# A gated feed-forward layer on one NeuronCore: where the second batch's x is loaded, and where the last sum of sign blocks stands in its slot

## The chip, the cores and the metric

The kernel runs on 1 core of one Trainium2 chip. The metric is the device time of one execution in microseconds (us). A profiled execution gives the span from the first to the last instruction of the program; the execution's own time is a little longer than that span.

## The reference, cut to what matters

Four batches of 1024 tokens with 512 features each pass through one conditioned gated layer:

```
scale = cond @ norm_w.T + 1.0
ms = mean(x * x, axis=-1, keepdims=True)
h = x * (scale[:, None, :] * rsqrt(ms + 1e-6))
u = h @ up_w.T                        # 512 -> 2 * 2048
val, gate = split(u, 2, axis=-1)
h = val * gelu(gate, approximate=False)
hq = act_quant(h)                     # per token: round(h * 127 / max|h|), scaled back
wq = weight_quant(down_w)             # -1, 0, 1 times mean|down_w|
y = hq @ wq.T                         # 2048 -> 512
return y + x
```

Everything is float32 outside the kernel; x is 4 x 1024 x 512.

## The kernel before, in words

**Tiling.** The 2048 hidden features are cut into NJ = 16 groups of 128. One *slot* is the work on one group for one batch: the "up" product of 1024 tokens (two halves of 512) with the group's gate and value rows, a Gelu on ScalarE (ACT), and a multiplication on VectorE (DVE) that writes the slot of `H`. Batch 0 runs in 16 *plain* slots (`first_batch(j, sc)`, j = 3 to 15, with j = 0 to 2 written out ahead of it); there the up product is made of 12 float16 matmuls of 128x128 by 128x512 for a gate (`pg`) and 12 for a value (`pv`), for each half (`plain_half`). From batch 1 on a slot uses seven products of a Strassen-like scheme (`slot`, `product`).

**What else the plain slots of batch 0 do.** They prepare the weights that later batches reload: `w_load(j + 4)` brings a group's 512 KB of `up_w` (line L261), `w_range(j + 3)` takes its largest values on DVE (L269, L147, L275, L278), `w_scale` and `w_rows` scale it and split it into high and low float16 parts (ACT L295 and L319, DVE L320, and a transposing DMA L321), `s_sums` builds sums on GpSimd (POOL, L353 to L356), `s_all` splits them (ACT L365, POOL L369) and spills the result to `s_dram` (L373, three DMAs from group 8 on). They also round the down weights (`d_round`, DVE L439 and L440; `d_put`, ACT L449 and a transposing DMA L451 into `wd`).

**Batch 1's x.** From slot 6 on, four pieces `Tokens(1, a)` of 256 tokens are prepared, each in two slots. In the even slot 6 + 2a: `norm` (ACT L495, then POOL L466 and L467), `scale` (ACT L503, DVE L508), `sums` (POOL L516 to L519). In the odd slot after it: `high` (ACT L540), `low` (DVE L544), `turn` (a transposing DMA, L547). The load itself, 512 KB, is `Tokens.load` (L487), and `next_tokens(j)` issues it for the piece that begins in slot j + 1: in slots 7 and 9 near the front of the slot, behind `w_load`, in slots 5 and 11 late in it. Pieces 0, 2 and 3 share one buffer, tag `xn`; piece 1 uses `H[:, 11]`.

**What sets the order.** The order of each engine's instructions is written out by hand (`manual_schedule`): an engine runs its list in the order of the source. All transfers spoken of here are issued by SyncE's queue (SP) in that order, and an SP instruction that waits holds up all behind it. From slot 6 to slot 11 that order is: w10, spill 7, L321 of group 9, spill 8 (three); w11, x for slot 8, `wd`, turn 0, spill 9 (three), L321 of group 10; w12, spill 10, L321 of 11; w13, x for slot 10, `wd`, turn 1, spill 11, L321 of 12; w14, spill 12, L321 of 13; w15, `wd`, x for slot 12, turn 2. (w12 stands for the load of group 12.)

**PSUM banks.** A value product `pv` uses tag `E` with two banks. So the `pv` of a half waits for the DVE multiplication (L604) of the half two places before it.

**The down product of batch 0** is made in slots 10 to 13 of batch 1, one piece of 256 tokens in each (`Pair`, L832), from blocks of `wd` and four differences of them, T1 to T4. `d_sums((n,))` makes difference n, as two DVE subtractions of 128x1024 float8 elements (L462). `D_SUM_AT` gives each slot a tuple of those made early in the slot, behind `pair.sums()`, and a tuple of those made late, behind `pair.third`. T2 is read by `pair.third`, T3 by `pair.fourth`, T4 by `pair.fifth`. The planner in the loop over batches takes `D_SUM_US` for every difference off the slot's DVE time, early or late.

```
D_SUMS = [("T1", "B12", "B11"), ("T2", "B22", "T1"), ("T3", "B22", "B12"), ("T4", "B21", "T2")]
D_SUM_AT = {(1, 9): ((0,), (2,)), (1, 10): ((1,), (3,))}
TOKENS = {6: 0, 8: 1, 10: 2, 12: 3}
```

Of the kernel before, what the change touches and what calls it, by code (L numbers as in the profile page):

```python
# [8 lines left out]
F32 = mybir.dt.float32  # L9
# [9 lines left out]
P = 128  # L19
# [31 lines left out]
def glu_quant_kernel(  # L51
# [14 lines left out]
    TOK = 512  # L66
# [10 lines left out]
    wpool = ctx.enter_context(tc.tile_pool(name="work", bufs=2))  # L77
# [16 lines left out]
    H = cpool.tile([P, NSLOT, 2, TOK], F32, name="H")  # L94
# [45 lines left out]
    def h_slots(g, n=1):  # L140
        s = g % NSLOT
        return H[:, s : s + n]
# [73 lines left out]
    def cond_spread(dg, b0, b1, tag):  # L216
        n = b1 - b0
        pd = bank(tag, {"po": 3}.get(tag, 2), [P, B], f"pd_{b0}")[:, :n]
        PE.matmul(pd, ones[:n, :], dg, start=True, stop=True)
        return pd  # L220

    def cond_undo(pd, b0, b1):
        DVE.reciprocal(ux[:, b0:b1], pd)
        if b0 == 0:
            DVE.tensor_scalar(scT[:, :, 0], scT[:, :, 0], ux[:, 0:1], None, ALU.mult)
        DVE.tensor_copy(dx[:, b0:b1], pd)

    def cond_rows():

        for b in range(1, B):  # L230
            SP.dma_start(out=rows_dram[b].rearrange("(k p) -> p k", p=P), in_=scT[:, :, b])
# [27 lines left out]
    def w_load(j, ts=(1, 0)):  # L259
        if j > 2:  # L260
            SP.dma_start(out=wn(j), in_=up_v[j])  # L261
            return
        for t in ts:
            SP.dma_start(out=wn(j)[:, t], in_=up_v[j][:, t])

    def w_largest(j, t0=0, t1=2):
        t = slice(t0, t1)
        am = sm.tile([P, 2], F32, name=f"wam_{j}_{t0}", tag="wam")[:, t]
        DVE.tensor_reduce(am, wn(j)[:, t], AX.X, ALU.max, apply_absolute_value=True)  # L269
        return am  # L270
# [9 lines left out]
    def w_range(j, t0=0, t1=2):  # L280
        w_factor(j, w_largest(j, t0, t1), t0, t1)

    def w_gain(j):
        DVE.tensor_scalar(sg0[:, j, :], sw[:, j, :], dx[:, 0:1], None, ALU.mult)
# [5 lines left out]
    def w_scale(j, ts=(1, 0), eng=None):  # L290
        eng = eng or (ACT if j >= ROWS else POOL)
        for t in ts:
            w, r = wn(j)[:, t], iv[j][:, t : t + 1]
            if eng is ACT:
                ACT.activation(w, w, AF.Copy, scale=r)  # L295
            else:
                eng.tensor_scalar(w, w, r, 1.0, ALU.mult, ALU.mult)
# [49 lines left out]
    def s_sums(j):  # L347
        if j >= ROWS:
            v = wn(j).rearrange("p t (n f) -> p t n f", n=2)
            a11, a12, a21, a22 = v[:, 1, 0], v[:, 1, 1], v[:, 0, 0], v[:, 0, 1]  # L350
        else:
            a11, a12, a21, a22 = (wf(j)[:, n] for n in range(4))
        POOL.tensor_tensor(sf[:, 0], a21, a22, ALU.add)  # L353
        POOL.tensor_tensor(sf[:, 2], a11, a21, ALU.subtract)
        POOL.tensor_tensor(sf[:, 1], sf[:, 0], a11, ALU.subtract)
        POOL.tensor_tensor(sf[:, 3], a12, sf[:, 1], ALU.subtract)  # L356
# [61 lines left out]
    def d_load(n):  # L418
        c, u, _ = d_at(n)
        SP.dma_start(out=d_part(n), in_=down_w[c * P : (c + 1) * P, u * HF : (u + 1) * HF])  # L420
# [5 lines left out]
    def d_total():  # L426
        part = sm.tile([P, 1], F32, name="wpart", bufs=1)
        DVE.tensor_reduce(part, wsum, AX.X, ALU.add)
        return part
# [39 lines left out]
    class Tokens:  # L469


        def __init__(self, b, a, at=None, nx_at=None):
            self.b, self.a = b, a
            if at is None:
                if a == 1:
                    self.xn = H[:, 11]
                else:
                    self.xn = wpool.tile([P, 2, D], F32, name=f"xn_{b}_{a}", tag="xn", bufs=1)
                self.xt = wpool.tile([P, 4, HALF], F32, name=f"xt_{b}_{a}", tag="xt", bufs=1)
            else:  # L480
                v = h_slots(at, 2)
                self.xn = v[:, 0]
                self.xt = v[:, 1].rearrange("p h (n d) -> p (h n) d", n=2)
            self.nx_at = nx_at
# [111 lines left out]
    def plain_half(j, h, between=nothing):  # L596
        pg = bank(*(("A", 2) if h or j == 1 else ("B", 1)), name=f"pg_{j}_{h}")
        plain(j, 1, h, pg)
        t1 = wpool.tile([P, TOK], F32, name=f"g_{j}_{h}", tag="t1")
        ACT.activation(t1, pg, AF.Gelu, scale=gain(j, 1))  # L600
        between()
        pv = bank("E", 2, name=f"pv_{j}_{h}")
        plain(j, 0, h, pv)
        DVE.scalar_tensor_tensor(h_half(j, h), pv, gain(j, 0), t1, ALU.mult, ALU.mult)  # L604
# [80 lines left out]
    def pair_max(b, i, h):  # L685

        v = h_slots(b * NJ + 2 * i, 2)[:, :, h].rearrange("p j t -> p t j")
        m = m_view(b, h)
        if i == 0:
            return [lambda: DVE.tensor_reduce(m, v, AX.X, ALU.max, apply_absolute_value=True)]  # L690
        gm = []

        def largest():
            gm.append(wpool.tile([P, TOK], F32, name=f"gm_{b}_{i}_{h}", tag="gm", bufs=1))
            DVE.tensor_reduce(gm[0], v, AX.X, ALU.max, apply_absolute_value=True)  # L695

        return [largest, lambda: DVE.tensor_tensor(m, m, gm[0], ALU.max)]  # L697
# [260 lines left out]
    am = w_largest(0, 1, 2)  # L958
# [39 lines left out]
    TOKENS = {6: 0, 8: 1, 10: 2, 12: 3}  # L998
# [4 lines left out]
    toks = {}  # L1003

    def next_tokens(j):
        if j + 1 in TOKENS:
            toks[j + 1] = toks[j + 2] = Tokens(1, TOKENS[j + 1])
            toks[j + 1].load()

    def s_all(j):  # L1010
        s_high(j)
        s_low(j, POOL)
        s_spill(j)

    def first_batch(j, sc):

        if j + 4 < NJ:
            w_load(j + 4)
        for n in D_LOAD.get(j, ()):
            d_load(n)  # L1020
        if j in (7, 9):
            next_tokens(j)
        t = toks.get(j)
        odd = t is not None and j not in TOKENS
        n = j + 2
        rows = ROWS <= n < NJ
        if j + 1 < ROWS:
            s_sums(j + 1)
        elif rows:
            s_sums(n)  # L1030
        if j + 3 < NJ:
            w_range(j + 3)
            w_gain(j + 3)
        if j == 5:
            part = d_total()
        if j + 3 < ROWS:
            w_scale(j + 3)
        plain_half(j, 0)
        if j == 3:
            pd = cond_spread(dg, 1, B, "po")  # L1040
            cond_undo(pd, 1, B)
            cond_rows()
        pairs = PAIRS.get(j, ())
        for i, h in pairs[:2]:
            for f in pair_max(0, i, h):
                f()
        if j + 1 < ROWS:
            s_all(j + 1)
        if n < ROWS:
            w_turn(n)  # L1050
            w_high(n)
            w_evac(n)
            w_low(n)
        if t and not odd:
            t.norm()
        for m in D_ROUND.get(j - 1, ()):
            d_put(m)
        for m in D_ROUND.get(j, ()) if j > 5 else ():
            d_round(m)
        if t and not odd:  # L1060
            t.scale(sc)
            t.sums()
        if odd:
            t.high()
            t.low(DVE)
        if j not in (7, 9):
            next_tokens(j)
        if odd:
            t.turn()
        plain_half(j, 1)  # L1070
        if j == 5:
            d_mean(part)
        if rows and j + 1 >= ROWS:
            s_all(n)
        if ROWS <= j + 3 < NJ:
            w_scale(j + 3)
            w_rows(j + 3)
        if rows and j + 1 < ROWS:
            s_sums(n)
            s_all(n)  # L1080
        if j == 5:
            d_round(0)
        for i, h in pairs[2:]:
            for f in pair_max(0, i, h):
                f()
        for n in D_SUM.get(j, ()):
            d_sum(n)
        if j in (NJ - 3, NJ - 1):
            s_load_x(NJ + (j - NJ + 3) // 2)
            s_load_y(NJ + (j - NJ + 3) // 2)  # L1090
# [99 lines left out]
    DOWN = {10: 0, 11: 1, 12: 2, 13: 3}  # L1190
    SLOT_US = 9.07
    PAIR_US = 6.2 - 5.1
    D_SUM_AT = {(1, 9): ((0,), (2,)), (1, 10): ((1,), (3,))}
    D_SUM_US = 2.3
    OWN_US = 3.0

# [71 lines left out]
    for b in range(1, B):  # L1268
        dve, act = Filler(), Filler()
        gains(b)  # L1270
        am = am_tile(b - 1)
        dq = state[b - 1] = sm.tile([P, 2 * NA], F32, name=f"dq_{b}", tag="dq")
        last_pair = NJ // 2 - 1
        for h in range(2):
            add_pair(
                dve, act, b - 1, last_pair, h, (0, "xz"[h]),
                lambda now, h=h: token_max(b - 1, h, am),
# [36 lines left out]
        for j in range(NJ):  # L1314
            g = b * NJ + j
            down = b + 1 < B and j in DOWN
            if down:
                pair, a = pairs[j], DOWN[j]
                xrs = [down_load(b - 1, h, a) for h in range(2)]
            early_sums, late_sums = D_SUM_AT.get((b, j), ((), ()))  # L1320
            left = SLOT_US + PAIR_US * down - OWN_US + 0.4
# [77 lines left out]
    b = B - 1  # L1399
    am = am_tile(b)  # L1400
# [158 lines left out]
```

## Time and profile before

| | us |
|---|---|
| three runs | 739.97, 740.22, 744.1 |
| their median | 740.22 |
| the profiled execution, own time | 740.59 |
| its span | 738.8 |
| TensorE busy (matmul) | 725.0 |
| VectorE busy | 592.3 |
| ScalarE busy | 390.8 |
| GpSimd busy | 201.4 |

The granted TensorE clock is full in all 40 slices of the page. A plain slot's four products of 12 matmuls take 2.59 us each. Slot 6 begins at 86.6 us, slot 8 at 107.85, slot 10 at 128.6, slot 12 at 151.75; the second batch begins at 195.1 us, and its slots 9 and 10 lie from about 269 to 301 us. Busy shares are averages; what a stage costs is read from the waits of TensorE in it and from what came last before each of them.

### The profile page before, as it was taken

The page shows a single profiled execution, that of the slowest core. Times are in us where ns is not written, and L with a number is a line of the kernel's source. Part 1 is how long each engine was busy: PE and PEld are TensorE (multiplying, and loading weights), DVE is VectorE, ACT ScalarE, POOL GpSimd, SP SyncE. Part 2 cuts the span into 40 slices and gives each one's busy share as a digit, 9 for nine tenths or more (in the row PEclk, how much of TensorE's full clock was granted, in tenths as well). Part 3 has the DMA queues.
Part 4 walks back from the last instruction along what each step waited for, and adds up shares of the span by engine and source line. Part 5 has one row for each costly group of instructions (what it writes and reads, how often), then busy time and mean ns, then how long its engine had stood idle before and what let it go on. Part 6 is the DMA issues. An engine that isn't in the chain of part 4 may idle for free.

```text
span 738.8 us, 10217 instructions
## 1 busy us (share of the span) xinstructions
PE 725.0 (98%) x3700; PEld 363.2 (49%) x3700; DVE 592.3 (80%) x837; ACT 390.8 (53%) x639; POOL 201.4 (27%) x217
## 2 busy tenths in 40 slices
PE   7999999899999999999999999999999999999998
PEld 3545444344444445565444445666444444445844
DVE  6968687986989888897679898687678888764897
ACT  5757657566235676443434666453433665332274
POOL 1499467787010031460010030452020000000100
PEclk9999999999999999999999999999999999999999
DMA  6289849999623456757933446656933335444253
GB/s 235 75 314 189 255 142 248 255 232 206 215 89 105 127 104 173 184 139 179 225 103 102 135 101 171 157 146 165 227 103 103 106 97 106 107 103 98 88 185 114
DMA packets 163022, 114.68 MB, mean 155 GB/s; under 512 B 124950, under 2 KB 129943, under 8 KB 162972
## 3 DMA queue, kind: packets, MB, share of 16 engines
q1 hardware_dynamic: 162682, 113.70, 58.3%
q8 instruction: 29, 0.48, 0.3%
q10 hardware_dynamic: 290, 0.33, 0.1%
q14 instruction: 21, 0.17, 0.1%
HBM read 62.08 MB, written 23.09 MB: 115 GB/s over the span
## 4 chain that ended last, share of the span: by engine, by line
PE 92%; DMA 2%; DVE 2%; ACT 1%; POOL 1%; issue 1%; SPq 0%; DVEq 0%; ACTq 0%
PE A L561 33%; PE E L561 17%; PE pv L576 9%; PE pg L576 8%; PE B L561 8%; PE po L832 8%; PE po_end L781 4%; DMA H<-in_L_cond_up_w_dram 1%; PE pw L305 1%; PE po L781 1%; DMA H<-in_x_dram 1%; PE ptx L922 1%; PE po_B L832 0%; DVE wd L462 0%; PE pv L619 0%
## 5 line engine op out<-in xcount | busy, mean ns | idle before, releaser
L561 PEld LDWEIGHTS <-SXY 128*128 128x128 f16 x2016 | 197.2, 98 | 232.3 <-issue 0.6
L561 PE MATMUL A<-R,SXY 128*128 128x512 f16 x1152 | 266.2, 379 | 0.0
L561 PE MATMUL E<-R,SXY 128*128 128x512 f16 x576 | 140.0, 379 | 0.1
L659 DVE SCALAR_TENSOR_TENSOR H<-A,sg,t 128x512 f32<-128x512 f32 x48 | 36.0, 750 | 74.2 <-PE A L561 74.0
L711 POOL PARTITION_ALL_REDUCE am<-R x8 | 14.3, 1793 | 231.1 <-DVE R L697 231.1
L753 DVE TENSOR_TENSOR H<-H,am 128x1024 f32<-128x1024 f32 x64 | 76.2, 1217 | 0.0
L672 ACT ACTIVATE t<-t,sg 128x512 f32<-128x512 f32 x48 | 34.6, 721 | 70.9 <-DVE t L669 70.7
L576 PEld LDWEIGHTS <-SXY 128*128 128x128 f16 x438 | 42.9, 98 | 55.2 <-issue 4.8
L561 PE MATMUL B<-R,SXY 128*128 128x512 f16 x288 | 70.0, 379 | 0.0
L695 DVE TENSOR_REDUCE gm<-H 128x512 f32<-128x1024 f32 x56 | 69.0, 1232 | 1.0
L832 PE MATMUL po<-wd,R 128*128 128x256 fp8e4 (+1 forms) x448 | 56.9, 275 | 1.4 <-DVE wd L462 1.4
L576 PE MATMUL pg<-R,SXY 128*128 128x512 f16 x252 | 57.8, 379 | 0.0
L832 PEld LDWEIGHTS <-R 128*128 128x128 bf16 (+1 forms) x480 | 46.9, 98 | 14.5 <-DVE wd L462 1.9
L466 POOL TENSOR_SCALAR ssq<-ssq 128x2 f32<-128x2 f32 x12 | 4.2, 349 | 179.9 <-ACT xt L495 127.5
L656 ACT ACTIVATE t<-B,sg 128x512 f32<-128x512 f32 x48 | 33.0, 687 | 36.5 <-PE B L561 36.5
L576 PE MATMUL pv<-R,SXY 128*128 128x512 f16 x186 | 45.4, 379 | 4.0 <-DVE H L604 4.0
L639 ACT COPY t<-A 128x512 f32<-128x512 f32 x48 | 27.9, 582 | 39.5 <-PE A L561 39.2
L647 ACT COPY B<-A 128x512 f32<-128x512 f32 x48 | 27.4, 572 | 38.3 <-PE A L561 37.8
L576 PEld LDWEIGHTS <-R 128*128 128x128 f16 x306 | 29.9, 98 | 35.7 <-issue 0.6
L761 ACT ACTIVATE H<-H 128x1024 f32<-128x1024 f32 x38 | 39.9, 1050 | 14.2 <-DVE H L753 11.1
L576 PE MATMUL pv<-R 128*128 128x512 f16 x186 | 45.4, 379 | 0.0
L651 ACT COPY v<-E 128x512 f32<-128x512 f32 x48 | 28.1, 585 | 31.3 <-PE E L561 27.8
(200 smaller groups left out, 1016.1 us busy)
## 6 DMA issues: line engine op xcount, KB each, us to landing
SXY<-s_dram SPq DMA_DIRECT2D x72, 256.0 KB, 3.2
SXY<-s_dram SPq DMA_DIRECT2D x24, 384.0 KB, 3.2
H<-in_L_cond_up_w_dram SPq DMA_DIRECT2D x13, 512.0 KB, 7.2
s_dram<-SXY SPq DMA_DIRECT2D x6, 896.0 KB, 5.7
xr<-in_x_dram SPq DMA_DIRECT2D x19, 256.0 KB, 3.0
out_dram<-xr SPq DMA_DIRECT2D x19, 256.0 KB, 2.4
H<-in_x_dram SPq DMA_DIRECT2D x9, 512.0 KB, 5.5
R<-in_L_cond_down_w_dram SPq DMA_DIRECT2D x8, 512.0 KB, 6.8
```

Of the source, the lines that this page charges most:

```text
L561: PE.matmul(o, s[:, w, k, :], tv[:, :, c, l, k, :], start=start and n == 0, stop=stop and n == len(TERMS) - 1, skip_group_check=True,)
L576: PE.matmul(ps, a[k // 2][:, w, k % 2, :], XP[:, l, k, h * TOK : (h + 1) * TOK], start=n == 0, stop=n == len(terms) - 1,)
L639: ACT.copy(cur["t2"], cur["A"])
L651: ACT.copy(cur["v"], cur["E"])
L656: ACT.activation(cur["t1"], pb, AF.Gelu, scale=gain(g, 1))
L659: DVE.scalar_tensor_tensor(h_half(g - 1, 0), prev["A"], gain(g - 1, 0), prev["t1"], ALU.mult, ALU.mult)
L672: ACT.activation(prev["t2"], prev["t2"], AF.Gelu, scale=gain(g - 1, 1))
L695: DVE.tensor_reduce(gm[0], v, AX.X, ALU.max, apply_absolute_value=True)
L753: DVE.tensor_tensor(v, v, r.to_broadcast([P, 2, TOK]), ALU.mult)
L761: ACT.activation(v, v, AF.Copy, bias=MAGIC)
L781: PE.matmul(po.rearrange("p (y c o) -> p y c o", c=2, o=P), q[:, a, h, j], wd8[:, :, j // n, j % n, :, y0:y1].rearrange("p c o y -> p y c o"),
L832: PE.matmul(po, w[:, j], m, start=start and j == 0, stop=stop and j == n - 1, skip_group_check=True,)
```

## The change

Three edits. First, `next_tokens(j)` issues the load for the piece that begins in slot j itself, and is called with j + 2 behind `w_load` at the front of each slot from 6 on (and with 6 in slot 5, at its old place). The load for slot 8 moves from slot 7 to slot 6, that for slot 10 from slot 9 to slot 8, that for slot 12 from slot 11 to slot 10; that for slot 6 stays. Second, pieces 1 and 3 get a buffer of their own in place of `H[:, 11]` and of the shared one: a tile of the tag `am`, which has one buffer and is used for `am` from batch 1 on. Third, T4 is made early in slot 10 of batch 1, behind T2, instead of behind `pair.third`.

```diff
             if at is None:
-                if a == 1:
-                    self.xn = H[:, 11]
+                if b == 1 and a % 2:
+                    v = wpool.tile([P, 2 * TOK], F32, name=f"xa_{b}_{a}", tag="am", bufs=1)
+                    self.xn = v.rearrange("p (h d) -> p h d", h=2)
                 else:
...
     def next_tokens(j):
-        if j + 1 in TOKENS:
-            toks[j + 1] = toks[j + 2] = Tokens(1, TOKENS[j + 1])
-            toks[j + 1].load()
+
+        if j in TOKENS:
+            toks[j] = toks[j + 1] = Tokens(1, TOKENS[j])
+            toks[j].load()
...
-        if j in (7, 9):
-            next_tokens(j)
+        if j > 5:
+            next_tokens(j + 2)
...
-        if j not in (7, 9):
-            next_tokens(j)
+        if j == 5:
+            next_tokens(6)
...
-    D_SUM_AT = {(1, 9): ((0,), (2,)), (1, 10): ((1,), (3,))}
+    D_SUM_AT = {(1, 9): ((0,), (2,)), (1, 10): ((1, 3), ())}
```

No instruction is added or taken out on any engine. On SP the three loads move up (by 6 places for slot 8, by 5 for slot 10, by 6 for slot 12, the three DMAs of a spill counted singly); on DVE the two subtractions of T4 move ahead of six others (L659, three of L544, two of L872). Nothing else changes its place.

## The prediction

> **What bounds the kernel now.** I read the page first, then the waits of TensorE (PE), then the chain of waits around each of them, then the timeline of SP's queue and of DVE.
>
> The page:
>
> ```profile
> span 738.8 us, 10217 instructions
> PE 725.0 (98%) x3700; PEld 363.2 (49%) x3700; DVE 592.3 (80%) x837; ACT 390.8 (53%) x639; POOL 201.4 (27%) x217
> ```
>
> PE has work for 725.0 of 738.8 us, and the change takes no matmul away. So only PE's idle time, 13.8 us, can be won. The waits of PE (who for whom: us in total, times, longest), from 70 to 200 us and then from 200 us to the end:
>
> ```profile
> PE pv L576 <- DVE H L604: 4.0, 2, 2.3
> PE pg L576 <- ACT g L600: 0.4, 1, 0.4
> ```
>
> ```profile
> PE po L832 <- DVE wd L462: 1.4, 1, 1.4
> ```
>
> What the change can reach is 4.0 + 0.4 + 1.4 = 5.8 us; the rest lies in the first 70 us, which it leaves alone. The two waits of `pv` are in slot 10 (2.26 us, before 133.62) and slot 12 (1.79 us, before 156.29). The chain that ended last, around them (start, us, what):
>
> ```profile
> 123.61 0.75 SPq L321
> ...
> 124.41 5.38 DMA H<-in_L_cond_up_w_dram
> ...
> 129.81 1.23 DVE wam L269
> ...
> 132.83 0.75 DVE H L604
> ...
> 133.62 2.75 PE pv L576 x12
> ...
> 146.75 1.73 SPq L321
> ...
> 148.53 4.10 DMA H<-in_L_cond_up_w_dram
> ...
> 155.50 0.75 DVE H L604
> ```
>
> Both waits end in the same way: SP comes late to w12 (124.41) and w14 (148.53); DVE stands at `w_range` until the weights land; behind it in DVE's list stands the multiplication L604 that frees the `E` bank. From landing to the end of L604 the chain is fixed: 129.81 to 133.58 is 3.8 us. SP's timeline shows why it is late:
>
> ```profile
> 110.96 0.51 SPq L487 DMA_DIRECT2D H<-in_x_dram  x1
> 111.57 1.24 SPq L451 DMA_TRANSPOSE wd<-tn  x1
> 114.16 4.86 SPq L547 DMA_TRANSPOSE R<-nx  x1
> ...
> 135.56 0.48 SPq L487 DMA_DIRECT2D xn<-in_x_dram  x1
> 136.09 1.25 SPq L451 DMA_TRANSPOSE wd<-tn  x1
> 137.68 5.70 SPq L547 DMA_TRANSPOSE R<-nx  x1
> ```
>
> A transposing DMA holds SP for as long as it cannot be handed on: turn 0 for 4.86 us, turn 1 for 5.70, while a turn at 327.26, with idle DMA engines before it, took 4.21. In the stretches of 2 us from 110 to 128 us the DMA engines are 0.93 to 1.34 busy, so what is queued there is paid in time. The x loads stand just ahead of these turns.
>
> **The change part by part.**
>
> *x for slots 8, 10 and 12.* At their new places they cost SP nothing: it issues w10 until 92.02 and then waits for POOL until 93.19, w12 until 126.53 and then until 130.25, w14 until 149.11 and then until 152.91. The issue takes 0.4 to 0.5 us (without that cover, so much each). No buffer holds them up: the `am` tile is free until batch 1, and the readers of piece 1 end with L544 at 137.65, before 149. The DMA engines are 0.53 busy in 128:130 and 0.17 in 152:154, so the transfers behind w12 and w14 find room.
>
> *Stall in slot 10.* Without x ahead of it, turn 0 still cannot start before 114.16, since DVE's L544 ends at 114.13. It takes 4.21 instead of 4.86 at best if only its own issue counts: SP comes to w12 0.65 earlier. 512 KB at the 346 GB/s of 110:112 is 1.5 us of DMA time that also leaves the queue ahead of w12's data, an estimate from that row. The gain ends where another gate takes over: DVE's L320 just before `w_range` ends at 128.03, 1.78 before the landing. So w12 is worth at most 1.78, and at worst it comes 0.8 later (if it now lands with the x behind it, as a pair that took 6.2 in slot 9, worked out below); I take 1.2, between 0.65 and 1.78. The stall becomes 2.26 - 1.2 = 1.06.
>
> *Stall in slot 12.* What is gated by the first stall comes 1.2 earlier: L544 ends at 136.45. SP now binds: w13 to 135.50, `wd` 1.25, so turn 1 starts at 136.85 in place of 137.68, 0.8 earlier. It had w13, x and `wd` ahead of it and took 5.70; turn 0 took 4.86 with w11, x and `wd` ahead, a lone one 4.21; I take 4.8, so 0.9 less. w14 is issued 1.7 earlier, and lands at 152.63 - 1.7 = 150.9. Next gate: L320 ends at 151.37; its ACT input waited for x in slot 10 (4.17 us, put down to a DVE that had long finished), but behind that POOL's `rsqrt` waits for `s_sums` until 141.4 in place of 142.63, so L320 moves only 1.2, to 150.2. The landing still comes last. L604 thus ends about 1.8 earlier (bounds: 2.9 later by the slower rival, 2.45 earlier with L320 as the gate), and this, not the sum of two gains, is what both stalls together give: 4.05 becomes 2.25.
>
> *Slots 12 to 15.* There PE does not wait, and must not begin to. L604 is ahead of the `pv` that needs it by 0.49 us in the second half of slot 12 (160.98 against 161.47), which moves with the same chain, then by 1.39 and 1.06. The 1.06 hangs on ACT's wait of 5.32 us for x at 165.02, which goes; POOL's sums end at 164.05, so `rsqrt` moves from 166.45 to about 164 at the same schedule, more than PE's 1.8. The 0.35 us stall before slot 8 hangs on POOL and ACT in slot 7, which stay: nothing.
>
> *T4 early.* DVE, PE and POOL in slot 10 of batch 1:
>
> ```profile
> 287.77 2.36 DVE L462 TENSOR_TENSOR wd<-wd 128x1024 fp8e4<-128x1024 fp8e4 x2
> 291.72 0.75 DVE L659 SCALAR_TENSOR_TENSOR H<-A,sg,t 128x512 f32<-128x512 f32 x1 [1.59 <-PE A L561]
> 295.24 4.27 DVE L462 TENSOR_TENSOR wd<-wd 128x1024 fp8e4<-128x1024 fp8e4 x2
> ```
>
> ```profile
> 299.57 2.03 PE L832 MATMUL po<-wd,R 128*128 128x256 fp8e4 x16 [1.39 <-DVE wd L462]
> ```
>
> T4 takes 4.27 beside POOL's L505 (294.96 to 298.43), T2 takes 2.36 while POOL rests. Behind T2 it runs from 290.13 to 292.5, with 1.59 of it in DVE's idle time; L659 and what follows shift by 0.8, and PE waits for none of them. Next late is the sum of the following piece, L808, needed 0.86 + 0.97 us (fifth product, first product) after PE's 298.2, so by about 300.0: from 292.5 DVE has L659 0.75, L544 2.2, L872 0.87, L669 0.68, L872 0.73, L808 0.68, ending at 298.4. It has 1.6 to spare, so the whole 1.39 goes. If what slowed T4 beside L505 now hits L544 and L808 in turn (up to 1.7 each, half of L505's 3.47), PE waits 3.4 - 1.6 = 1.8, 0.4 more than now: bounds -0.4 and 1.4. I take 1.3, by the row of T2. PE's first product of the following piece, which the wait for T4 covered, gets a wait of its own for L872 (its bank): due at 296.3, needed at 299.06.
>
> The Trainium skill (SBUF — State Buffer, Who interferes with whom) says that a DVE instruction with two SBUF inputs and a GpSimd instruction that reads SBUF shut each other out for the length of the instruction. The rows 2.36 and 4.27 agree, but the same rule also reaches L544 and L808, which speaks against the move; by it alone the gain would be anything from -0.4 to 1.4.
>
> *Sum.* -1.8 - 1.3 = -3.1 us. The profiled execution was 740.59 with a span of 738.8, so 1.8 lies around the span, and it is 0.37 over the median. 740.22 - 3.1 is about 737.1.
>
> The Trainium skill (DMA: Bandwidth & Descriptors, Issuing engines are not separate DMA queues) speaks against the loads' new places: all transfers run on the same 16 engines and interleave, so x right behind w12 and w14 would slow them. By that rule the sum is the slower rival's. The trace speaks otherwise: w13, with x issued 0.63 behind it at 135.56, was read by DVE at 139.92, at most 4.99 after its issue; w12 with nothing behind it took 5.38.
>
> **The rivals.**
>
> *The weights land as before.* A lone turn still takes 4.21 and L321 3.2 in most slots, so SP may lose elsewhere what it wins, and only T4 counts: 740.22 - 1.3 = 738.9. For it: w12's issue alone took 2.12 us, whatever was ahead. Against it: DMA saturated from 110 to 128 us. 20%.
>
> *Both stalls close.* If w12 gains its full 1.78 and w14 the 2.45 or more, and ACT's missing waits pull L320 further: 740.22 - 4.0 - 1.4 = 734.8. Against it POOL, busy without a break from 124.78 to 141.4. 14%.
>
> *Only T4's wait comes back, as the lock on L808.* 740.22 - 1.8 = 738.4. 8%.
>
> *Slower: x shares the engines with the load ahead of it.* In slot 9 w13 and x together took 6.2 us from w13's issue to x's landing at 141.13. If w12 and w14 land only so, they come 6.2 - 5.38 = 0.8 and 6.2 - 4.10 = 2.1 later; with no faster turn that adds up along the chain to 2.9, less T4's 1.3: 741.8. It decides from where w14's landing loses more than the 1.7 + 1.3 won. The row of w13 is against it. 8%.
>
> **How the numbers follow.** The forecast, both parts acting, has 50%: 737.1, between 736.2 and 738.1 by its halves. The range takes in T4 alone (738.9) above, with 0.5 for the measurement, and most of the way to the closed stalls below: 735.3 to 739.4; the slower case and part of the closed one are left out, under 2 in 10. One per cent, 7.4 us, is about what a measurement of this kernel can tell from no change. A gain of 7.4 exceeds the 5.8 in reach: 0.02. A loss of it needs more than twice the slower rival's price: 0.03. Within: 0.95.
>
> **What would show it.** x loads at about 92, 126 and 148 us on SP, no wait of ACT's L495 for x; turns 0 and 1 shorter; w12 and w14 issued 0.7 to 1.8 earlier; PE's waits for L604 together near 2.2 us; T4 at 2.4 us directly behind T2 and no wait of PE for L462. I am wrong if the turns still take 4.9 and 5.7 us, if w12 or w14 takes over 6 us to land, or if PE waits in slots 13 to 15.

## The result and the profile after

The changed kernel took 738.91 us (median of 20 runs, 737.66 to 742.2), the kernel before 742.09 beside it (20 runs, 739.97 to 744.58). The ratio is 0.9961, 95% interval 0.9948 to 0.9973. Put on the 740.22 us that the prediction starts from, it gives 737.3; 737.1 was predicted. The time came out, but not its working: three terms were taken too large and one was missing. Measured once more (`after_again`, below) the ratio is 0.9977, a gain of 1.7 us where this one gives 2.9, so the agreement to 0.2 us is partly luck.

The lines of the changed kernel's code are one higher than before from L476 on (the multiplication L604 is now L605, the value product L576 is L577, L808 is L809). Its page, and below it the waits of TensorE (the first three from 70 to 200 us, the last from 200 us to the end):

```profile
span 736.1 us, 10215 instructions
PE 725.4 (99%) x3700; PEld 363.4 (49%) x3700; DVE 591.9 (80%) x837; ACT 390.6 (53%) x639; POOL 198.6 (27%) x217
```

```profile
PE pv L577 <- POOL H L355: 1.6, 1, 1.6
PE pv L577 <- DVE H L605: 1.3, 1, 1.3
PE pg L577 <- ACT g L601: 0.4, 1, 0.4
...
PE po L833 <- DVE H L809: 0.6, 1, 0.6
```

The waits of the value products in slots 10 and 12 are 1.58 and 1.29 us instead of 2.26 and 1.79. The 1.58 is put down to POOL, but its product starts 0.05 us after the multiplication L605 ends, as before. The 0.4 before slot 8 has stayed. T4's 1.39 is gone, and a wait of 0.62 that was not there has come. The spans differ by 2.71 us: 1.18 from the two stalls, 1.39 - 0.62 = 0.77 from T4, and 0.76 from the time before slot 6, which the change does not touch. What differs there is a wait for the first loads (1.10 us at 10.4 us, 2.19 before); it was between 1.1 and 3.2 us in fourteen profiles, so this last part is not the change's.

SP's timeline, at the loads and turns:

```profile
113.40 4.26 SPq L548 DMA_TRANSPOSE R<-nx  x1
...
123.11 1.61 SPq L261 DMA_DIRECT2D H<-in_L_cond_up_w_dram  x1
124.78 0.46 SPq L488 DMA_DIRECT2D xn<-in_x_dram  x1
...
136.20 5.12 SPq L548 DMA_TRANSPOSE R<-nx  x1
...
146.45 0.58 SPq L261 DMA_DIRECT2D H<-in_L_cond_up_w_dram  x1
147.08 0.48 SPq L488 DMA_DIRECT2D xa<-in_x_dram  x1
```

Turn 0 took 4.26 us (4.86 before), turn 1 5.12 (5.70), and x stands behind w12 and w14. DVE in slots 10 and 12 of the second batch, and the products of the down projection there:

```profile
285.82 4.63 DVE L462 TENSOR_TENSOR wd<-wd 128x1024 fp8e4<-128x1024 fp8e4 x4
...
324.27 1.76 DVE L698 TENSOR_TENSOR R<-R,gm 128x512 f32<-128x512 f32 x1
...
328.00 1.22 DVE L809 TENSOR_TENSOR H<-R 128x1024 bf16<-128x1024 bf16 x1
```

```profile
296.07 2.02 PE L833 MATMUL po<-wd,R 128*128 128x256 fp8e4 x16
...
329.28 1.05 PE L833 MATMUL po<-wd,H 128*128 128x256 fp8e4 x8 [0.62 <-DVE H L809]
```

T2 and T4 together take 4.63 us, so T4 costs 2.3 and not 4.27, and the product that waited for it (296.07) waits for nothing. The new wait is two slots later.

### The profile page after: what moved, and what is told of

It reads as the page before. It is cut to its first block, busy times and chain, and to the rows that moved or that the text cites. A ratio compares the mean times of both kernels' runs of the same rounds, so it can differ in the third digit from the quotient of the medians.

```text
span 736.1 us, 10215 instructions
## 1 busy us (share of the span) xinstructions
PE 725.4 (99%) x3700; PEld 363.4 (49%) x3700; DVE 591.9 (80%) x837; ACT 390.6 (53%) x639; POOL 198.6 (27%) x217
## 4 chain that ended last, share of the span: by engine, by line
PE 92%; POOL 3%; DVE 2%; ACT 1%; issue 1%; DMA 1%; SPq 0%; DVEq 0%; POOLq 0%; ACTq 0%
PE A L562 34%; PE E L562 17%; PE B L562 8%; PE po L833 8%; PE pv L577 8%; PE pg L577 8%; PE po_end L782 4%; PE pw L305 1%; PE po L782 1%; DMA H<-in_x_dram 1%; POOL SXY L369 1%; PE ptx L923 1%; PE po_B L833 0%; PE pv L620 0%; ACT H L295 0%
## 5 line engine op out<-in xcount | busy, mean ns | idle before, releaser
L577 PEld LDWEIGHTS <-SXY 128*128 128x128 f16 x438 | 42.8, 98 | 54.0 <-issue 3.6
L577 PE MATMUL pg<-R,SXY 128*128 128x512 f16 x252 | 57.8, 379 | 0.0
L577 PE MATMUL pv<-R,SXY 128*128 128x512 f16 x186 | 45.4, 379 | 2.9 <-POOL H L355 1.6
L577 PEld LDWEIGHTS <-R 128*128 128x128 f16 x306 | 29.9, 98 | 35.7 <-issue 0.6
L577 PE MATMUL pv<-R 128*128 128x512 f16 x186 | 45.4, 379 | 0.0
```

What stands on the lines that cost most here:

```text
L577: PE.matmul(ps, a[k // 2][:, w, k % 2, :], XP[:, l, k, h * TOK : (h + 1) * TOK], start=n == 0, stop=n == len(terms) - 1,)
```

## The experiments

Times in the tables are us after the first product of slot 8, so that what happened earlier drops out. "Multiplication" is the start of the one that frees the bank for the first value product of the slot.

**The two parts alone, and both kernels again.** `t4_only` is the kernel before with the last line of the change:

```diff
-    D_SUM_AT = {(1, 9): ((0,), (2,)), (1, 10): ((1,), (3,))}
+    D_SUM_AT = {(1, 9): ((0,), (2,)), (1, 10): ((1, 3), ())}
```

> The kernel before with only the last sum of signs (T4) moved to the front of its slot. Theory A (the two parts are separate and add up): TensorE's wait of 1.39 us for L462 goes, its waits in slots 10 and 12 of batch 0 stay at 2.26 and 1.79 us, and the time falls by 0.8 to 1.4 us, ratio 0.998 to 0.999. Theory B (the change's whole gain comes from the x loads): ratio 1.000. Theory C (the 0.62 us wait for the sum L808 two slots later is a price of the earlier T4): that wait shows up here too, and the net gain is about 0.8 us.

`loads_only` is the changed kernel without that line:

```diff
-    D_SUM_AT = {(1, 9): ((0,), (2,)), (1, 10): ((1, 3), ())}
+    D_SUM_AT = {(1, 9): ((0,), (2,)), (1, 10): ((1,), (3,))}
```

> The changed kernel with T4 back at its old place. Theory A: the wait of 1.39 us for L462 is there; TensorE's waits in slots 10 and 12 are near 1.6 and 1.3 us as in the changed kernel (2.26 and 1.79 before); ratio 0.998 to 0.999. Theory B (the weights land as before, and what the changed profile shows is chance): 2.26 and 1.79 us, ratio 1.000. Theory C: no wait for the sum L808 in slot 12 of batch 1.

`after_again` and `before_again` are the two kernels unaltered.

> The changed kernel again, for what repeats in its profile. Theory A: waits near 1.6, 1.3 and 0.36 us in batch 0, none for L462; turn 0 near 4.3 us; ratio 0.995 to 0.998. If the 0.62 us wait for the sum L808 (slot 12 of batch 1) is chance, it is absent or of another size here; if it is built into the order, it comes again within 0.1 us.

> The kernel before again, for what repeats in its profile. Waits of 2.26, 1.79 and 1.39 us within 0.1 us if they are built into the order; the wait near the start (2.19 us before, 1.10 in the changed kernel's profile, in code that the change doesn't touch) may have any size from 1 to 2.5 us if it depends on when the first loads land.

| | ratio to before, 95% interval | median, us | span of the profile |
|---|---|---|---|
| t4_only | 0.9992 (0.9974 to 1.0009) | 741.21 | 739.1 |
| loads_only | 0.9978 (0.9960 to 0.9996) | 740.86 | 740.1 |
| after_again | 0.9977 (0.9959 to 0.9995) | 739.81 | 736.6 |
| before_again | a single run | 742.36 | 740.6 |

The waits at T4 are clear. Without the last line the 1.39 is there (loads_only, before_again); with it, it is gone and the 0.6 stands in slot 12 (t4_only, after_again). So the new wait belongs to T4's part, and T4 is worth 0.78 us by the traces; the timed ratio of t4_only does not tell it from nothing. POOL in the changed kernel shows why:

```profile
323.58 3.59 POOL L506 TENSOR_TENSOR H<-H,sc 128x512 f32<-128x512 f32 x2 [1.12 <-ACT H L504]
```

In the kernel before, L697 (0.68 us, at 327.12) slipped in beside the first instruction of this pair (327.08). PE and POOL now come 3.5 us earlier there and DVE, without a gap, 2.85; L698 comes 0.7 us into that instruction and takes 1.76, and L809 behind it is late. It is 1.76 in all eight profiles with T4 early and 0.68 to 0.69 in all six without.

The stalls are less clear. In loads_only turn 1 took 5.66 us and the stalls 1.59 and 2.44, together as long as before (4.05). With the same loads the changed kernel gave 1.58 and 1.29, and 0.89 and 2.29 in after_again. Two things therefore had to be found: what decides inside a stall, and how much of the gain belongs to which load.

**One load at a time.** `x8_early` moves only x for slot 8, `x10_early` only x for slot 10; the last line of the change is left out in all three kernels of this set, the buffers are the changed kernel's, and in the first two x for slot 12 is loaded where it was before. `x_ahead` moves all three, but to the place just ahead of the weight load.

```diff
-        if j > 5:
-            next_tokens(j + 2)
+        if j == 6:                # x10_early: j == 7
+            next_tokens(8)
+        if j == 9:                # x10_early: j == 8
+            next_tokens(10)
...
-        if j == 5:
-            next_tokens(6)
+        if j in (5, 11):
+            next_tokens(j + 1)
```

> Loads-only kernel with only the load for slot 8 at its new place; those for slots 10 and 12 at their old ones. Times counted from the first matmul of slot 8. Theory A (what is won is SP's time behind each turn, turn by turn): turn 0 takes 4.3 us (4.9 to 5.1 in the kernel before), w12 is issued at 16.0 (16.6 to 16.9), turn 1 takes 5.7 to 5.9 as before, w14 is issued near 40.0 (40.6 to 40.9; 39.4 to 40.0 with all three moved). Theory D (the x loads moved one by one win nothing, it is the sum of the queue): w14 at 40.6 or later. Rival E (a load behind w12 slows it): not touched here, since nothing is behind w12; w12's read by DVE would come 0.3 us or more sooner after its issue than the 4.5 to 5.4 us with x behind it.

> Loads-only kernel with only the load for slot 10 at its new place. Theory A: turn 0 takes 4.9 to 5.1 us and w12 is issued at 16.6 to 16.9 as in the kernel before; turn 1 takes 5.1 to 5.6 and w14 is issued 0.3 to 0.6 earlier than before, near 40.2. Theory D: nothing moves. Rival E: w12, now with x behind it, is read 0.8 us later than before (22.0 to 22.8 from slot 8's start).

```diff
+        if j > 5:
+            next_tokens(j + 2)
         if j + 4 < NJ:
             w_load(j + 4)
...
-        if j > 5:
-            next_tokens(j + 2)
```

> Loads-only kernel with each x load issued directly ahead of its slot's weight load instead of behind it. Theory A (transfers of one queue run in their order, so what stands ahead costs its whole transfer and what stands behind costs next to nothing): w12 and w14 are read by DVE 1.5 to 2 us later than with x behind: near 22.8 and 45.3 from slot 8's start; the waits in slots 10 and 12 grow to 3 and 2 us or more. Rival E (they share the engines, so the order hardly matters): read within 0.5 us of the loads-only kernel's 21.3 and 43.5 to 44.5.

They took 741.52, 740.38 and 743.28 us in a single run each (spans 739.7, 738.6, 741.5), and the traces say more:

| | turn 0 | w12 issued | multipl., slot 10 | turn 1 | w14 issued | multipl., slot 12 | waits, slots 10 / 12 |
|---|---|---|---|---|---|---|---|
| before | 4.86 | 16.56 | 24.98 | 5.70 | 40.68 | 47.65 | 2.26 / 1.79 |
| t4_only | 5.07 | 16.92 | 24.32 | 5.93 | 40.64 | 47.60 | 1.60 / 2.41 |
| x8_early | 4.24 | 15.93 | 23.63 | 5.88 | 40.64 | 47.58 | 0.90 / 2.92 |
| x_ahead | 4.28 | 16.62 | 25.00 | 4.67 | 40.34 | 47.71 | 2.27 / 1.82 |
| loads_only | 4.30 | 16.04 | 24.32 | 5.66 | 39.97 | 47.64 | 1.59 / 2.44 |
| x10_early | 5.01 | 16.87 | 24.32 | 5.10 | 39.40 | 46.48 | 1.59 / 1.28 |
| after | 4.26 | 16.03 | 24.30 | 5.12 | 39.36 | 46.47 | 1.58 / 1.29 |
| after_again | 4.26 | 16.00 | 23.63 | 5.29 | 39.43 | 46.79 | 0.89 / 2.29 |

Three readings. First, what slot 10 gains alone is lost in slot 12: x8_early shortens the first stall by 1.36 us and the second grows by 1.13; the multiplication of slot 12 comes 0.07 earlier, no more, and w14 is issued at 40.64 where 40.0 was expected. Nor is the step in slot 10 the load's alone: t4_only, with the loads of before, has it at 24.32 too. Second, x10_early by itself gives the multiplication of slot 12 the place that it has in the changed kernel (46.48 against 46.47), without x for slots 8 or 12. The loads' whole gain here is that one move, by a turn 1 that is 0.6 us shorter and starts 0.7 earlier. Third, x right behind a weight load costs that load next to nothing: from w14's issue to its reading by DVE it is 4.0 to 4.1 us with x behind in five of six profiles (4.5 in loads_only) and 4.0 to 4.1 in the five without. (For w12 it is 4.5 to 5.6 with and 4.3 to 5.4 without, which tells nothing.) Ahead of it, it costs 0.6 us of SP for its issue and, at w14, 0.8 us of the landing (4.91 us to the reading), and x_ahead has both stalls back, although its turns are short. Its w12 was read at 21.90, not at the 22.8 that a whole transfer ahead of it would have meant.

**The weights ahead of the turns.** `w_before_turn` is the changed kernel, with w12 and w14 issued at the end of slots 7 and 9, ahead of turn 0 and turn 1:

```diff
-        if j + 4 < NJ:
+        if j + 4 < NJ and j not in (8, 10):
             w_load(j + 4)
...
         if j == 5:
             next_tokens(6)
+        if j in (7, 9):
+            w_load(j + 5)
         if odd:
             t.turn()
```

> The changed kernel, with w12 issued in slot 7 ahead of turn 0 and w14 in slot 9 ahead of turn 1, in place of the front of slots 8 and 10. Theory A (the weights' landing is what both waits in batch 0 still end with): DVE reads w12 and w14 without waiting for a load; the next gate is DVE's L320 (21 and 42 us from slot 8's start, where the kernel waits until 21.4 and 43.5), so the two waits of TensorE together fall from 2.9 to about 1.2 us, ratio to the kernel before 0.994 to 0.996. Theory F (DVE, ACT and POOL are as late as the weights): the waits stay at 2.5 us or more, ratio 0.996 to 0.998. If the turns, now 0.6 us later each, hold up the spills behind them, the waits move to slots 11 to 13.

It took 738.38 us (737.06 to 739.94), ratio 0.9933 (0.9916 to 0.9951). w12 is issued at 5.23 instead of 16.03 and has landed before DVE wants it (of the profile, the slowest of the six runs, only what follows slot 8's start is read; a wait of 2.59 us before slot 8, 0.3 to 0.6 in all others, arose before either of the weight loads that this edit moves): `w_range` starts at 20.10, right behind L320. The stall of slot 12 is gone, though 0.51 us stands in slot 13, the second batch begins at 85.07 (86.10 in the changed kernel, 87.29 before), and yet slot 10 still waits 0.91. That tells what decides inside the stall. All engines in the kernel before, of which DVE's and POOL's rows are shown:

```profile
130.81 0.72 POOL L353 TENSOR_TENSOR H<-H 128x256 f32<-128x256 f32 x1
...
131.06 0.49 DVE L147 TENSOR_SCALAR wam<-wam 128x2 int32<-128x2 int32 x1
...
131.49 0.72 POOL L354 TENSOR_TENSOR H<-H 128x256 f32<-128x256 f32 x1
131.59 0.65 DVE L275 TENSOR_SCALAR sw<-wam 128x2 f32<-128x2 f32 x1
...
132.17 0.72 POOL L355 TENSOR_TENSOR H<-H 128x256 f32<-128x256 f32 x1
...
132.35 0.56 DVE L284 TENSOR_SCALAR sg<-sw,dx 128x2 f32<-128x2 f32 x1
132.83 0.74 DVE L604 SCALAR_TENSOR_TENSOR H<-pv,sg,g 128x512 f32<-128x512 f32 x1
```

and in w_before_turn, with the product that waits in the last row:

```profile
130.30 1.21 DVE L269 TENSOR_REDUCE wam<-H 128x2 f32<-128x1024 f32 x1
...
130.93 1.65 POOL L369 TENSOR_TENSOR SXY<-H,SXY 128x768 f16<-128x768 f32 x1
...
131.54 1.06 DVE L147 TENSOR_SCALAR wam<-wam 128x2 int32<-128x2 int32 x1
...
132.53 0.67 POOL L369 TENSOR_TENSOR R<-H,R 128x256 f16<-128x256 f32 x1
...
132.64 0.59 DVE L275 TENSOR_SCALAR sw<-wam 128x2 f32<-128x2 f32 x1
133.16 0.72 POOL L353 TENSOR_TENSOR H<-H 128x256 f32<-128x256 f32 x1
...
133.35 0.57 DVE L284 TENSOR_SCALAR sg<-sw,dx 128x2 f32<-128x2 f32 x1
...
133.83 0.74 DVE L605 SCALAR_TENSOR_TENSOR H<-pv,sg,g 128x512 f32<-128x512 f32 x1
...
134.62 0.38 PE L577 MATMUL pv<-R,SXY 128*128 128x512 f16 x1 [0.91 <-POOL H L354]
```

L147, L275 and L284 work on two elements a partition. They take 0.17 to 0.2 us where POOL rests. Here each ends 0.02 to 0.04 us after a POOL instruction ends: L147 at 131.55 with L353 (131.53), L275 at 132.24 with L354 (132.21), L284 at 132.91 with L355 (132.89); in w_before_turn they end with the two L369 and L353. In all fourteen profiles each of the three ends 0.02 to 0.05 us behind a POOL instruction. Three such steps have to be taken behind `w_range`, and POOL's train of 0.68 us steps gives them their times. So the multiplication of slot 10 has three places in all profiles with this order: 24.98 to 25.01, 24.30 to 24.32, or 23.63. They belong to a `w_range` that starts at 21.9 to 22.1, at 21.2 to 21.5, or at 20.1 to 20.8; between 20.8 and 20.1 an earlier landing buys nothing. No run moves POOL's instructions instead, so that POOL is what sets these times is read from the ends, not tried.

The Trainium skill (SBUF — State Buffer, Who interferes with whom) has the lock between DVE and GpSimd, and counts `tensor_scalar` in the 2-port modes among what takes it. The three steps agree, with 1.06 us for L147 where it needs 0.17.

**The multiplication ahead of `w_range`.** `mult_first` is the changed kernel with DVE's list changed in slots 9 and 11:

```diff
-        if j + 3 < NJ:
+        if j + 3 < NJ and j not in (9, 11):
             w_range(j + 3)
             w_gain(j + 3)
...
         plain_half(j, 0)
+        if j in (9, 11):
+            w_range(j + 3)
+            w_gain(j + 3)
```

> The changed kernel, with w_range of groups 12 and 14 (L269 to L284) put behind the multiplication L605 in DVE's list in slots 9 and 11. Theory (the multiplication is late only because it stands behind w_range, which waits for the weights and then for POOL's s_sums): it runs at about 20.2 us after slot 8's first product instead of 24.30, and TensorE's wait in slot 10 goes from 0.9 to 1.6 down to 0.3 or less. The next multiplication, behind three L545, is then due 1.6 earlier than before, so in slot 12 a wait of up to 2 us may stand before the second value product instead of the first. Start of the second batch 84.5 to 86.1 after slot 8 (86.10 to 86.43 in the changed kernel). Rival (it is late for a reason of its own, its value product or Gelu): the wait in slot 10 stays at 0.9 to 1.6.

All engines in its slot 10:

```profile
128.27 0.75 DVE L605 SCALAR_TENSOR_TENSOR H<-pv,sg,g 128x512 f32<-128x512 f32 x1
...
129.80 1.22 DVE L269 TENSOR_REDUCE wam<-H 128x2 f32<-128x1024 f32 x1 [0.79 <-DMA H<-in_L_cond_up_w_dram]
...
131.52 2.75 PE L577 MATMUL pv<-R,SXY 128*128 128x512 f16 x12
...
137.15 0.74 DVE L605 SCALAR_TENSOR_TENSOR H<-pv,sg,g 128x512 f32<-128x512 f32 x1
...
137.94 0.59 PE L577 MATMUL pv<-R,SXY 128*128 128x512 f16 x2 [1.09 <-DVE H L605]
```

`w_range` still waits 0.79 us for the weights, but the multiplication runs at 128.27, at 20.10 after slot 8's start instead of 24.30, and the first value product (131.52) waits for nothing. The rival is out: the multiplication had no reason of its own to be late. Of the stall, 1.09 us comes back at the second value product of slot 10 and 0.62 at that of slot 12, behind the three L545. The second batch begins at 84.94. A single run took 737.8 us; seven more:

> The kernel of the first look with w_range behind the multiplication, timed. If DVE's order is worth what its trace showed (the second batch 1.1 to 1.5 us earlier than in the changed kernel), its ratio to the kernel before lies about 0.0015 to 0.002 below the changed kernel's 0.9961, at 0.994 to 0.9947, and at full granted clock it takes 737.2 to 737.8. Rival (the look was a fortunate execution): 0.996 or above, 738.4 to 738.7 at full clock.

737.42 us (737.05 to 740.04), ratio 0.9942 (0.9917 to 0.9966). Its trace has the second batch at 85.00, with the waits at other places (0.68 us in slot 11, 1.09 in slot 12). The interval of the ratio reaches that of the changed kernel; what sets it apart is the trace and the runs at full clock, below.

**The sum earlier, and all together.** `sum_first` is the changed kernel with L809 of the following piece behind the third product's work:

```diff
-                mid = [lambda: (pair.third(xrs, dq), d_sums(late_sums)), lambda: (pair.fourth(), next_pair()), lambda: (loads(), pair.fifth())]
+                mid = [lambda: (pair.third(xrs, dq), d_sums(late_sums), next_pair()), lambda: (pair.fourth(),), lambda: (loads(), pair.fifth())]
```

> The changed kernel, with the sum L809 of the following piece made right behind the third product's work instead of behind the fourth's, in slots 10 to 12 of batches 1 and 2. Theory (the new wait of 0.6 in slot 12 of batch 1 is DVE being late, because L698 took 1.76 and L809 1.22 beside POOL's scale of the next x): L809 runs about 1.5 us earlier and the wait for it goes; the span is 0.6 lower if nothing takes its place, the same if a wait for L872 or for ACT's t of 0.4 to 0.8 does. Rival (the wait is one for the bank, put down to L809): a wait of 0.6 stays at the same product.

`mult_and_w` has this, the order of mult_first and the early weights of w_before_turn.

> w12 and w14 issued ahead of the turns, w_range behind the multiplication in slots 9 and 11, and the sum L809 earlier, on top of the changed kernel. Theory (SP's order and DVE's order together are the whole of both stalls): waits of TensorE between slots 10 and 13 together below 0.7 us (2.9 to 3.2 in the changed kernel, 1.4 with the weights alone moved); start of the second batch about 83.5 after slot 8's first product (85.07 with the weights alone moved); about 2 us below the changed kernel at the same granted clock, 736.5 to 737.5. Rival (DVE and POOL, not the weights, set the pace of slots 8 to 12): the waits come back a slot or a half later, start at 85 or more, time 738 to 739.

sum_first took 740.22 us in a single run (span 738.4): the wait for L809 is gone and one of 0.39 for L873 stands in its place, so 0.2 us is won. mult_and_w took 738.14 us (736.59 to 740.36), ratio 0.9953 (0.9935 to 0.9972). Here the theory fell, and the numbers are the rival's: waits of 0.93 (slot 11) and 0.80 (slot 13) come back, 1.73 in all where less than 0.7 was expected, and the second batch begins at 85.24, no earlier than with either half alone. The rival's cause holds in part only. Both waits end with a multiplication behind the `w_range` of groups 13 and 15, whose loads and places in DVE's list no run here moves: DVE stands there 2.71 us for ACT's L319, which comes behind POOL's sums, and then 0.21 and 0.80 us for the weights themselves.

**The clock.** Each run lists the mean granted clock of TensorE, and it was not the same in all. Some profiles show why. The stretches of 2 us around slot 12's stall in t4_only (PEclk is the eighth column, 1.00 is full), and the value product that follows the stall:

```profile
154.00:156.00 2.00, 0.35 (x2) 0.11 (x2) 1.97 (x5) 1.20 (x3) 1.79 (x4) 0.93 0.99 303
156.00:158.00 2.00, 2.00 (x6) 0.75 (x5) 2.00 (x3) 1.97 (x4) 2.00 (x2) 0.50 1.15 213
158.00:160.00 2.00, 2.00 (x8) 0.82 (x7) 2.00 (x3) 1.07 (x2) 2.00 (x2) 0.71 0.86 169
160.00:162.00 2.00, 2.00 (x11) 0.91 (x10) 2.00 (x3) 0.00 (x0) 2.00 (x3) 1.00 1.19 239
```

```profile
155.65 4.44 PE L576 MATMUL pv<-R,SXY 128*128 128x512 f16 x12 [2.41 <-DVE H L604]
```

Behind the wait of 2.41 us the clock is halved for 3.41 us, and the twelve matmuls take 4.44 us in place of 2.75: 1.7 us. In fourteen profiles 7 of the 11 waits of 2.28 to 3.17 us brought such a drop: three in slot 12 (t4_only, loads_only, x8_early), three at the first loads (before_again, sum_first, x_ahead), one in slot 10 (before_again). None of the 28 waits of 1.09 to 2.27 us (the 1.43 at the very start left out) did.

The length alone does not decide: the stall of slot 10 brought no drop with 2.26 us (before) and one with 2.28 (before_again), and 2.73 us at the first loads brought none (mult_first_timed). What decides is where the wait falls. Every drop lasts 3.41 us, and the two of before_again begin at 12.23 and 135.11 us, 36 times 3.413 apart; in five more traces a stretch of half clock behind TensorE's last product lies 171, 213 or 214 times 3.413 behind the drop. So the clock is set in windows of 3.413 us that run on through the program. Two of them, each with the window behind it (PE's busy time is the third column), show a drop and none:

```profile
131.70:135.11 3.41, 1.29 (x6) 0.48 (x5) 3.31 (x6) 2.07 (x3) 3.33 (x6) 1.00 0.70 246
135.11:138.52 3.41, 3.25 (x8) 1.13 (x8) 3.41 (x4) 3.38 (x6) 3.27 (x4) 0.50 1.19 187
```

```profile
153.10:156.51 3.41, 1.58 (x8) 0.75 (x8) 3.38 (x6) 2.28 (x4) 3.20 (x4) 1.00 1.06 282
156.51:159.92 3.41, 3.41 (x18) 1.52 (x17) 3.41 (x4) 2.73 (x6) 3.41 (x4) 1.00 1.07 233
```

The first pair is before_again's stall of 2.28 us, of which 2.12 lie in one window; the second is after_again's of 2.29, of which only 1.83 do. In the eleven traces that show the windows' phase, each of the seven windows ahead of a drop has TensorE busy for 0.10 to 0.38 of it, and none of the other 2348 up to TensorE's last product has it below 0.46. So 2.1 us of waiting within one window brought a drop, and 1.8 us brought none; a longer wait that falls across two windows need not bring one. The Trainium skill (TensorE: Matmul & The Clock Gate, What's actually happening) has half clock after an idle window of about 3.4 us that runs free of the program; the window and its luck agree, but it need not be idle throughout, since 0.38 busy was little enough here.

A drop of 3.41 us at half clock lowers the mean over the run by 0.5 x 3.41 / 740 = 0.0023, so a mean of 0.998 is one drop and 0.995 two. Runs by their mean, with the median of those at 1.000:

| | 0.999 and above | 0.997, 0.998 | 0.995 and below | median at 1.000, us (runs) |
|---|---|---|---|---|
| before, 66 runs beside the experiments | 16 | 30 | 20 | 740.21 (14) |
| t4_only | 4 | 4 | 4 | 739.71 (4) |
| loads_only | 6 | 5 | 1 | 739.80 (5) |
| after and after_again | 17 | 6 | 4 | 738.70 (14), 738.46 (1) |
| w_before_turn | 4 | 1 | 1 | 737.93 (4) |
| mult_and_w | 6 | 6 | 0 | 737.30 (4) |
| mult_first, both | 6 | 2 | 0 | 737.25 (4), 737.80 (1) |

The medians of before under the first three headings are 740.25, 742.06 and 744.29 us, so about 2 us go with each drop. The changed kernel's runs have fewer drops, and with the stalls at 1.1 us or less (mult_first) no run has two. These rows are from several chips, and the runs of before beside the result have no clock on record; 5 of those 20 lie below 741 us, as 15 of the 16 under the first heading do. At full clock the change is worth 740.21 - 738.70 = 1.5 us; the measured 2.9 us (0.39% of 742.09; 2.0 to 3.9 by the interval) has fewer drops in it, by the table about 1.1 a run before and 0.5 after, which at 1.7 us each is 1.0 us more. That split is an estimate from these rows: which wait brought a drop is not recorded in timed runs, and the wait for the first loads, which no edit here touches, brings some too. In after_again's set the measured gain is 1.7 us, which leaves little to split. At full clock mult_first is another 1.4 us below the changed kernel.

## Why the prediction was right in its time and wrong in three terms

*x at its new places.* Right. SP issued it at 91.33, 124.78 and 147.08, under the waits named, and no wait was added.

*The stall in slot 10.* Turn 0 took 4.26 where 4.21 was given as the floor, and w12 was issued 0.53 us earlier (0.5 to 0.7 in the profiles with x for slot 8 early): the floor of 0.65 was the whole of it. The "1.5 us of DMA time" that was to leave the queue ahead of w12's data, and made 1.2 of 0.65, bought nothing to be seen. The next gate was named as L320; by the profiles it is POOL's train with the three small DVE steps, which moves the multiplication by 0.68 or not at all. The stall became 1.58, or 0.89 in another execution, where 1.06 was given.

*The stall in slot 12.* The chain was right and the size was not. Turn 1 started 0.72 us earlier (0.8 predicted) but took 5.12 and not the 4.8 taken; w14 was issued 1.3 earlier (1.7), and the multiplication came 1.18 earlier (1.8). "This, not the sum of two gains, is what both stalls together give" was right, and x8_early and x10_early show it best. The term that was mis-sized is turn 1's 0.9: it lost 0.6. Both stalls became 2.87 us, with 2.25 predicted; loads_only shows an execution in which nothing was won, with a turn 1 of 5.66; why that turn was long stays open.

*Slots 12 to 15 and the 0.35.* Right: no new wait there, and 0.36 stayed.

*T4.* Its wait went whole, as predicted, and T4 ran at 2.3 us behind T2. "The whole 1.39 goes, I take 1.3" missed that the lock would be paid two slots later, where DVE has no gap: 0.62 came back, and 0.77 was left. The rival "only T4's wait comes back, as the lock on L808" had the right instruction, looked for it at the next piece, and took T4's whole gain for lost, where 0.62 of 1.39 was.

*The sum.* -1.8 - 1.3 = -3.1 was -1.2 - 0.8 = -2.0 in the trace and -1.5 at full clock. What most likely brings the measured ratio to -2.9 is a term that the prediction did not have: a stall of some 2.1 us or more can cost 1.7 more in half clock. The profiled execution of before showed full clock in all 40 slices because its stall of 2.26 fell across two windows; in before_again the same stall brought a drop. That 737.3 came so close to 737.1 is luck in part: terms 1.1 us too large met one that was missing, and after_again gave -1.7.

*The other rivals.* "The weights land as before" is out by x10_early. "Both stalls close" needed more than early weights: w_before_turn still waits 0.91 in slot 10. "x shares the engines with the load ahead of it" is out: w14 is read 4.0 to 4.1 us after its issue without x behind it, and with it in five of six profiles.

## What to carry to other kernels

When a chain of waits ends in a list, ask first whether the late instruction has to stand behind the one that waits: swapping two entries in DVE's list twice brought the second batch forward by 1.1 to 1.2 us, as much as moving three transfers had (1.2). A gain in one stall is worth what the next stall does not take back, so cost a pair of them from the last one. And a stall has a second price in the clock that follows it, paid in some executions and not in others; read the granted clock of several, for one may show none of it.

## What the runs showed of the hardware that was not expected

- DVE instructions on 128x2 elements took 0.17 us alone and up to 1.06 beside POOL. In slot 10 the three in a row ended 0.02 to 0.05 us behind a POOL instruction in all fourteen profiles.
- The clock of TensorE was halved for 3.41 us behind 7 of 11 waits of 2.28 us and over: where TensorE was busy for 0.38 or less of one of the windows of 3.413 us that run on through the program.
- A transposing DMA held SP for 4.2 to 5.2 us (turn 0) and 4.7 to 6.2 (turn 1) with transfers of the same size. Turn 0 took 4.2 to 4.3 us with no load just ahead of it, 4.9 to 5.1 with x there, and 5.0 and 5.2 with w12 there (w_before_turn, mult_and_w).
